# Scaling and sums of the down-projection weights: from one early block to short pieces placed along the feed-forward chunks

## The chip, the cores and the metric

The kernel runs on one core of a Trainium2 chip. The metric is the device time of one launch in microseconds (us). TensorE (PE) does the matmuls, VectorE (DVE), ScalarE (ACT) and GpSimd (POOL) do elementwise work, and SyncE (SP) issues nearly all the DMA transfers. The engines run side by side, each through its own list of instructions in a fixed order, and wait for each other through semaphores.

## The reference

One post-norm transformer layer on x of shape (2, 512, 512) in float32. The attention part is large; the change lies in the feed-forward part, whose weights come as int32 with a scale for each output:

```python
x = _layernorm(x + _L0_attn_ref(x, Wq, Wk, Wv, Wo, q_norm_w, k_norm_w))   # 32 heads, 8 kv heads, 128 wide
# feed-forward: D_MODEL = 512, D_FF = 1376
gate = silu(einsum('bsd,fd->bsf', x, gate_w.astype(f32)) * gate_s)
up   = einsum('bsd,fd->bsf', x, up_w.astype(f32)) * up_s
h    = gate * up
ffn  = einsum('bsf,df->bsd', h, down_w.astype(f32)) * down_s
x = _layernorm(x + ffn)
```

## The kernel before, in words

Both batches of 512 tokens stay in on-chip memory (SBUF) from start to end. Attention takes the first 80% of the time; from about 870 us on the feed-forward mixes in. Its gate and up projections are cut into 11 chunks of 128 features (the last has 96). Each chunk is computed for batch 0 and batch 1; "visit 9.1" below is chunk 9, batch 1. There are 22 visits: chunks 0 to 3 for batch 0, then chunks 4 to 10 for both batches, then chunks 0 to 3 for batch 1.

**Products.** A matrix product is done in a two-by-two block form with seven block products instead of eight (a Strassen-like scheme). Its operands are the blocks themselves and sums or differences of them. `PLAN` (line 546) lists the products in the order 1, 2, 6, 7, 4, 5, 3; they accumulate in three PSUM banks: 1, 6, 7 and 4 in bank a, 2 in bank c, 5 and 3 in bank b. After each product its bank is read out before the next product may write to it: `ffn_up` (line 1221) has ACT copy bank a into gu (line 640) and DVE add bank b or c to gu (`tensor`, line 513; line 518 in the profile). So product 6 waits for the copy after product 1, product 4 for the copy after product 7, and product 3 for the gu add after product 5, which itself needs the copy after product 7. When all seven are in, ACT computes the sigmoid (sg, line 1280) and DVE makes sg (line 1288) and hT (line 1297), the result of the visit. gu has two buffers: the first copy of a visit waits for hT of the visit before the last one.

**Operand sums.** For each chunk, the int32 weights wi come by DMA (line 1195), ACT or POOL cast them to wf, and four DVE or POOL operations make the weight sums sw (`sums_a`, line 523). wi, wf and sw have two buffers each. The sums over the tokens are tx. The down projection needs, for each pair of token tiles, sums sh over h, and once the differences td of its weights (`sums_b`, line 534): four operations on blocks of 5 chunks by 256 columns.

**Down weights.** They come as int32 in 11 pieces (wdi, line 1348, two buffers); DVE multiplies each by the output scale ds_sb into wd (128 x 512, in the loop of line 1342). Then `sums_b` makes td from wd in four operations of 1280 elements per partition. wd is first read by the down projection's products and by the 96-row rest (ps, line 1412), td by its later products.

**What sets the order.** The program doesn't write the order of the engines out by hand. Each operation is put on a list with an estimated cost for each engine that may do it, a priority, and the operations that it depends on. A planner (`Work.emit`, line 146) then plays the engines' clocks forward and emits at each step the operation that can start first, by estimated time and then by priority. The engine and the order are fixed by this at build time; the chip then only waits for data and for free buffers. An operation given in `after` counts as a dependence in the planner alone, and no semaphore comes of it. The estimates know nothing of engines slowing each other.

The priorities of the lines that change: the visits have `base + n` (n from 0 to 21), and

```python
base + 4.0 + fc      # load of wdi, piece fc
base + 4.5 + fc      # scaling of wd, piece fc
base + 16.0          # the four td differences
```

Of the kernel before, what the change touches and what calls it, by code (L numbers as in the profile page):

```python
# [26 lines left out]
NF = -(-DFF // P)  # L27
FL = DFF - (NF - 1) * P
KF = (NF - 1) // 2
# [3 lines left out]
WO = DM // 2  # L33
# [5 lines left out]
EARLY = 4  # L39
# [14 lines left out]
def act(n, scaled=False):  # L54
    return 0.15 + 0.00084 * n + (0.1 if scaled else 0.0)


def dve(n, sbuf=False):
    return 0.2 + 0.0014 * n if sbuf else 0.15 + 0.00106 * n


def pool_tt(n):
    return 0.28 + 0.0021 * n
# [168 lines left out]
def post_ln_block(  # L232
# [23 lines left out]
    W = Work()  # L256
# [18 lines left out]
    def fixed(ring_, name):  # L275
        return Buf(ring_, name)
# [51 lines left out]
    qw, kw = fixed(r_qw, "qw"), fixed(r_kw, "kw")  # L328
# [16 lines left out]

    def load(mb, prio, fn, writes, reads=(), queue="SP"):
        engine = {"SP": nc.sync, "ACTQ": nc.scalar}[queue]
        W.add({queue: mb / 0.3}, prio, lambda e: fn(engine), reads, writes)  # L350

    w_qkv, w_o = {}, {}

# [156 lines left out]

    def tensor(n, prio, dst, a, b, alu, reads, writes, who=("DVE", "POOL")):
        cost = {"DVE": dve(n, len(who) > 1), "POOL": pool_tt(n)}
        W.add(
            {e: cost[e] for e in who},
            prio,
            lambda e: vec[e].tensor_tensor(dst(), a(), b(), alu),  # L518
            reads,
            writes,  # L520
        )

    def sums_a(n, prio, s, a, s_key, a_keys):
# [7 lines left out]
        tensor(n, prio, g(1), g(0), f(0, 0), sub, [s_key(0)] + k(0, 0), [s_key(1)])  # L531
        tensor(n, prio, g(3), f(0, 1), g(1), sub, k(0, 1) + [s_key(1)], [s_key(3)])

    def sums_b(n, prio, t, b, t_key, b_keys):

        sub = ALU.subtract
        k = b_keys
        f = lambda r, c: (lambda: b(r, c))
        g = lambda j: (lambda: t(j))
        tensor(n, prio, g(0), f(0, 1), f(0, 0), sub, k(0, 1) + k(0, 0), [t_key(0)])  # L540
        tensor(n, prio, g(1), f(1, 1), g(0), sub, k(1, 1) + [t_key(0)], [t_key(1)])
        tensor(n, prio, g(2), f(1, 1), f(0, 1), sub, k(1, 1) + k(0, 1), [t_key(2)])
        tensor(n, prio, g(3), f(1, 0), g(1), sub, k(1, 0) + [t_key(1)], [t_key(3)])


    PLAN = [
# [90 lines left out]
    def copy_op(n, prio, dst, src, reads, writes, who=("ACT", "DVE")):  # L637
        def fn(e):
            if e == "ACT":
                nc.scalar.copy(dst(), src())  # L640
            else:
                vec[e].tensor_copy(dst(), src())  # L642

        cost = {"ACT": act(n), "DVE": dve(n), "POOL": 0.2 + 0.00095 * n}
        W.add({e: cost[e] for e in who}, prio, fn, reads, writes)
# [472 lines left out]
    for p in range(NP):  # L1118
        g, b, i = pairs[p]
# [96 lines left out]
        )  # L1216
        return wf, sw

    turn = [0]

    def ffn_up(fc, b, weights, prio):

        fw = min(P, DFF - fc * P)
        key = f"{fc}_{b}"
        wf, sw = weights
        gu, sg = Buf(r_gu, f"gu_{key}"), Buf(r_sg, f"sg_{key}")
        if b not in hT:
            hT[b] = Buf((r_h0, r_h1)[b], f"hT_{b}")
        h, xb, tb = hT[b], x1T[b], tx[b]
        homes = ((r_f, r_f, r_f), (r_sc, r_sc, r_po))[turn[0] % 2]  # L1230
        turn[0] += 1

        def copy(n, bank):
            copy_op(
                NTH,
                prio,
                lambda: gu[:fw, n, :],
                lambda: bank[:fw, :NTH],
                [A(bank)],
                [(gu, n)],  # L1240
                ("ACT",),
            )

        def add(n, bank):
            tensor(
                NTH,
                prio,
                lambda: gu[:fw, n, :],
                lambda: bank[:fw, :NTH],
                lambda: gu[:fw, n, :],  # L1250
                ALU.add,
                [A(bank), (gu, n)],
                [(gu, n)],
                ("DVE",),
            )

        def done(which, bank):
            if which == 1:
                copy(0, bank)
            elif which == 2:  # L1260
                add(0, bank)
            elif which == 6:
                copy(1, bank)
            elif which == 7:
                copy(3, bank)
            elif which == 5:
                add(3, bank)
            elif which == 4:
                copy(2, bank)
            else:  # L1270
                add(1, bank)
                finish()

        def finish():
            gcol, ucol = lambda: gs_sb[:fw, fc : fc + 1], lambda: us_sb[:fw, fc : fc + 1]
            gate = lambda: gu[:fw, 0:2, :].rearrange("p n c -> p (n c)")
            W.add(
                {"ACT": act(S, True)},
                prio,
                lambda e: nc.scalar.activation(sg[:fw, :], gate(), AF.Sigmoid, scale=gcol()),  # L1280
                [(gu, 0), (gu, 1), A(gs_sb)],
                [A(sg)],
                table="sigmoid",
            )
            W.add(
                {"DVE": 0.75},
                prio,
                lambda e: nc.vector.scalar_tensor_tensor(
                    sg[:fw, :], gate(), gcol(), sg[:fw, :], ALU.mult, ALU.mult
                ),  # L1290
                [(gu, 0), (gu, 1), A(gs_sb), A(sg)],
                [A(sg)],
            )
            W.add(
                {"DVE": 0.75},
                prio,
                lambda e: nc.vector.scalar_tensor_tensor(
                    h[:fw, fc, :],
                    gu[:fw, 2:4, :].rearrange("p n c -> p (n c)"),
                    ucol(),  # L1300
                    sg[:fw, :],
                    ALU.mult,
                    ALU.mult,
                ),
                [(gu, 2), (gu, 3), A(us_sb), A(sg)],
                [(h, (fc, 0)), (h, (fc, 1))],
            )

        def a_ap(f, ch):
            if isinstance(f, tuple):  # L1310
                return wf[:, f[0], 2 * f[1] + ch, :fw]
            return sw[:, f, ch, :fw]

        def a_keys(f):
            return [(wf, f[0])] if isinstance(f, tuple) else [(sw, f)]

        def b_ap(f, ch):
            if isinstance(f, tuple):
                return xb[:, 2 * f[0] + ch, f[1] * NTH : (f[1] + 1) * NTH]
            return tb[:, f, ch, :]  # L1320

        def b_keys(f):
            return [(xb, 2 * f[1]), (xb, 2 * f[1] + 1)] if isinstance(f, tuple) else [(tb, f)]

        seven(prio, Factor(a_ap, a_keys), Factor(b_ap, b_keys), fw, NTH, 2, f"h{key}", done, homes)


    base = NU + 3.0
# [3 lines left out]
    n = 0  # L1332
# [8 lines left out]
    wd, td = Buf(r_wd, "wd"), Buf(r_td, "td")  # L1341
    for fc in range(NF):
        fw = min(P, DFF - fc * P)
        wdi = Buf(r_wdi, f"wdi_{fc}")
        load(
            0.26,
            base + 4.0 + fc,
            lambda q, fc=fc, fw=fw, wdi=wdi: q.dma_start(
                wdi[:fw, :], dwt[fc * P : fc * P + fw, :]
            ),  # L1350
            [A(wdi)],
        )
        tensor(
            DM,
            base + 4.5 + fc,
            lambda fc=fc, fw=fw: wd[:fw, fc, :],
            lambda fw=fw, wdi=wdi: wdi[:fw, :],
            lambda fw=fw: ds_sb[:fw, :],
            ALU.mult,
            [A(wdi), A(ds_sb)],  # L1360
            [(wd, fc)],
            ("DVE",),
        )
    sums_b(
        KF * WO,
        base + 16.0,
        lambda j: td[:, j],
        lambda r, n: wd[:, KF * r : KF * r + KF, n * WO : (n + 1) * WO],
        lambda j: (td, j),
        lambda r, n: [(wd, KF * r + c) for c in range(KF)],  # L1370
    )

    def ffn_down(t, prio):
        b, i = divmod(t, NTB)
# [26 lines left out]
            return td[:, f, ch, :]  # L1401

        def b_keys(f):
            return [(wd, KF * f[0] + c) for c in range(KF)] if isinstance(f, tuple) else [(td, f)]


        for r in (0, 1):
# [4 lines left out]
                lambda e, r=r, bank=bank: nc.tensor.matmul(  # L1412
                    bank.tile,
                    lhsT=h[:FL, NF - 1, ts(i + r, P)],
                    rhs=wd[:FL, NF - 1, :],
                    start=True,
                    stop=True,
                ),
# [13 lines left out]
                ("DVE",),  # L1432
            )
        seven(prio, Factor(a_ap, a_keys), Factor(b_ap, b_keys), P, WO, KF, f"d{t}", done, homes)
        for r in (1, 0):
            o = Buf(r_o, f"o_{t + r}")
# [4 lines left out]
                lambda q, r=r, o=o: q.dma_start(out[ts(t + r, P), :], o.tile),  # L1441
# [54 lines left out]
```

## Time and profile before

| what | value |
|---|---|
| median of 3 runs | 1101.1 us (1099.43 to 1101.75) |
| the profiled execution's own time | 1100.44 us |
| its span, first to last instruction | 1098.5 us |
| mean granted PE clock | 0.995 |
| PE busy | 1073.0 us, 98% of the span |
| DVE, ACT, POOL busy | 676.1, 409.8, 485.2 us |
| scaling of wd on DVE | ten records of 128x512, 12.4 us in all, mean 1251 ns |
| td differences | three on POOL, mean about 3.1 us; one on DVE, 1.48 us |

The profile is of one execution. A line of the timeline gives start and length in us, the engine, the line of the source, the operation, the tile written and the tiles read, and in brackets the idle time before it with what ended it. "PEld" is PE's weight load. A matmul of one product of the feed-forward shows as four records in a row. A PE that is busy need not run at full speed: the granted clock is given beside it, with 1.00 as full.

### The profile page before, as it was taken

To read this page: it belongs to the slowest core of one execution; us is meant where nothing else is said; L and a number is where in the kernel's file an instruction comes from. 1 tells how busy PE (TensorE), PEld (TensorE's weight loads), DVE (VectorE), ACT (ScalarE), POOL (GpSimd) and SP (SyncE) were. 2 spreads that over 40 slices of the span, in tenths; PEclk is the share of its full clock that TensorE was granted. 3 is DMA by queue.
4 is the path that set the end of the run, shared out by engine and by line. 5 is a ranking of instruction groups with operands and counts; after the bars stand their busy time and mean duration, and the time that the engine had idled before them with its cause. 6 is when DMAs were issued, how large, how long until landed. Compare 5 with 4: busy or idle time off the path is not lost.

```text
span 1098.5 us, 13035 instructions
## 1 busy us (share of the span) xinstructions
PE 1073.0 (98%) x4548; PEld 764.7 (70%) x4548; DVE 676.1 (62%) x1553; ACT 409.8 (37%) x1015; POOL 485.2 (44%) x596
## 2 busy tenths in 40 slices
PE   8999999999999999999999999999999987999997
PEld 5667676767676666666676666666667775888886
DVE  8756565656564655465665656566666588557454
ACT  2543334344344434434333434344444332344100
POOL 9443444344543444335444445354656265224030
PEclk9999999999999999999999999999999998999999
DMA  9210011001100110011001100000101033111011
GB/s 281 74 58 1 1 39 58 1 1 39 58 1 1 38 58 1 1 39 58 1 1 39 58 1 16 23 1 1 39 1 39 20 88 92 33 40 38 1 39 39
DMA packets 44144, 38.92 MB, mean 35 GB/s; under 512 B 3664, under 2 KB 36432, under 8 KB 44080
## 3 DMA queue, kind: packets, MB, share of 16 engines
q1 hardware_dynamic: 42352, 37.05, 11.0%
q10 hardware_dynamic: 1728, 1.05, 0.4%
q8 instruction: 36, 0.59, 0.2%
q14 instruction: 28, 0.23, 0.1%
HBM read 35.99 MB, written 2.10 MB: 35 GB/s over the span
## 4 chain that ended last, share of the span: by engine, by line
PE 85%; DVE 7%; POOL 5%; DMA 1%; issue 1%; ACT 1%; SPq 0%; POOLq 0%; DVEq 0%
PE pa_q L565 13%; PE pa L965 10%; PE sc L874 10%; PE pa_o L565 9%; PE pt L942 6%; PE pb_q L565 6%; PE pa_h L565 6%; PE pb_o L565 5%; PE pc_q L565 4%; PE pb_h L565 3%; PE pa_d L565 3%; PE ptq L821 2%; DVE tq L518 2%; PE pc_o L565 2%; POOL inv L504 2%; POOL pr L923 2%
## 5 line engine op out<-in xcount | busy, mean ns | idle before, releaser
L923 POOL TENSOR_SCALAR pr<-pr,rden 128x32 f32<-128x32 f32 (+15 forms) x256 | 155.8, 627 | 148.6 <-DVE rden L914 148.0
L899 ACT ACTIVATE pr<-pr,nmax 128x32 f32<-128x32 f32 (+15 forms) x256 | 131.9, 516 | 95.4 <-DVE nmax L883 95.2
L965 PE MATMUL pa<-prT,v 128*128 128x512 f32 x320 | 164.2, 595 | 0.0
L874 PE MATMUL sc<-kT,qT 128*128 128x160 f32 (+15 forms) x512 | 149.0, 402 | 0.0
L883 DVE CUSTOM_DVE_ANT_0 pr<-sc,bias 128x32 f32<-128x32 f32 (+15 forms) x256 | 109.0, 436 | 28.0 <-PE sc L874 25.3
L874 PEld LDWEIGHTS sc<-kT,qT 128*128 128x128 f32 x512 | 90.4, 191 | 47.6 <-issue 29.6
L640 ACT COPY c<-pa_q 128x384 f32<-128x384 f32 x101 | 48.2, 477 | 135.4 <-PE pa_q L565 130.5
L942 PEld LDWEIGHTS pt<-ident,pr 128*128 128x128 f32 x640 | 76.4, 141 | 26.7 <-issue 9.7
L942 PE MATMUL pt<-ident,pr 128*128 128x128 f32 x640 | 91.5, 275 | 0.9 <-POOL pr L923 0.3
L565 PE MATMUL pa_q<-tq,sx 128*128 128x384 f32 x248 | 90.4, 487 | 1.4 <-POOL pr L923 1.4
L640 ACT COPY prT<-pt 128x512 f32<-128x512 f32 x107 | 60.4, 586 | 79.1 <-PE pt L942 79.0
L504 POOL TENSOR_TENSOR inv<-ms,nhalf 128x10 f32<-128x10 f32 x32 | 63.3, 1977 | 53.5 <-DVE ms L779 53.2
L518 DVE TENSOR_TENSOR y<-y,pa_o 128x256 f32<-128x256 f32 x128 | 53.6, 419 | 50.7 <-PE pa_o L565 49.9
L642 DVE COPY prT<-pt 128x512 f32<-128x512 f32 x53 | 36.2, 690 | 61.8 <-PE pt L942 61.7
L763 ACT ACTIVATE sq<-c 128x640 f32<-128x640 f32 x64 | 47.2, 737 | 69.6 <-DVE c L518 67.4
L518 DVE TENSOR_TENSOR c<-pb_q,c 128x384 f32<-128x384 f32 x62 | 34.3, 554 | 61.9 <-PE pb_q L565 58.1
L965 PEld LDWEIGHTS pa<-prT,v 128*128 128x128 f32 x320 | 56.7, 191 | 21.9 <-issue 4.9
L642 POOL COPY v<-c 128x128 f32<-128x128 f32 x50 | 16.1, 321 | 124.1 <-DVE c L518 124.1
L565 PE MATMUL pa_o<-to,so 128*128 128x256 f32 x256 | 65.9, 380 | 0.3 <-POOL pr L923 0.3
L565 PEld LDWEIGHTS pa_q<-tq,sx 128*128 128x128 f32 x248 | 46.0, 192 | 27.4 <-POOL pr L923 2.6
L565 PEld LDWEIGHTS pa_o<-to,so 128*128 128x128 f32 x256 | 47.1, 190 | 20.1 <-issue 9.9
L640 ACT COPY gu<-pa_h 128x256 f32<-128x256 f32 (+1 forms) x88 | 31.9, 370 | 78.1 <-PE pa_h L565 65.3
(152 smaller groups left out, 2060.3 us busy)
## 6 DMA issues: line engine op xcount, KB each, us to landing
w<-in_wqt_dram SPq DMA_DIRECT2D x32, 256.0 KB, 4.3
wo<-in_wot_dram SPq DMA_DIRECT2D x8, 1024.0 KB, 5.5
wi<-in_gwt_dram SPq DMA_DIRECT2D x14, 256.0 KB, 2.9
wi<-in_uwt_dram SPq DMA_DIRECT2D x14, 256.0 KB, 3.2
wdi<-in_dwt_dram SPq DMA_DIRECT2D x10, 256.0 KB, 2.7
y<-in_x_dram SPq DMA_DIRECT2D x1, 2048.0 KB, 13.1
out_dram<-o SPq DMA_DIRECT2D x8, 256.0 KB, 2.0
w<-in_wkt_dram SPq DMA_DIRECT2D x7, 256.0 KB, 4.9
```

Of the source, the lines that this page charges most:

```text
L504: lambda e: nc.gpsimd.tensor_tensor(dst(), src(), nhalf[:, :n], ALU.pow),
L518: lambda e: vec[e].tensor_tensor(dst(), a(), b(), alu),
L565: nc.tensor.matmul(bank[:rows, :width], lhsT=a(fa, c), rhs=b(fb, c), start=(fresh and c == 0), stop=(c == depth - 1), skip_group_check=True,)
L640: nc.scalar.copy(dst(), src())
L642: vec[e].tensor_copy(dst(), src())
L763: lambda e, r=r: nc.scalar.activation(sq[:, r].rearrange("p h d -> p (h d)"), c(r)[:, : 5 * HD], AF.Square),
L874: lambda e, a=a, w=w, sc=sc: nc.tensor.matmul(sc[:, :w], lhsT=qT[:, a, :, :], rhs=kT[:, :w], start=True, stop=True),
L883: lambda e, a=a, w=w, sc=sc: nc.vector.tensor_tensor_reduce(out=pr[:, a, :w], in0=sc[:, :w], in1=bg[:, S - w :], scale=-1.0, scalar=MAX_IN ...
L899: lambda e, a=a, w=w: nc.scalar.activation(pr[:, a, :w], pr[:, a, :w], AF.Exp, bias=nmax[:, a : a + 1], scale=-1.0, accum_out=den[:, a : a ...
L923: lambda e, a=a, w=w: nc.gpsimd.tensor_scalar(pr[:, a, :w], pr[:, a, :w], rden[:, a : a + 1], 1.0, ALU.mult, ALU.mult),
L942: nc.tensor.transpose(pt[:, ts(a, P)], pr[:, a, ts(j, P)], ident.tile)
L965: lambda e, j=j, prT=prT: nc.tensor.matmul(po.tile, lhsT=v[:, j, :], rhs=prT.tile, start=(j == 0), stop=(j == i)),
```

## The change

The planner is told more. Each wdi load and each wd scaling is held in the plan until a given visit is finished, and the td differences are cut from four operations of 5 x 256 into twenty of 256, four for each of five chunk pairs, each group held until a given visit is finished. `finished` collects, for each of the 22 visits, the operation that writes hT; `EARLY` is 4 and `NF` 11. So piece fc of wd may be planned once visit number 4 + fc (counted from 0) is done, its load one visit earlier, and group c of td once visit 15 + c is done. Besides, the cost that the planner assumes for a wd scaling is changed from that of a PSUM operation to that of an SBUF one (0.69 to 0.92 us by its formulas). The keys by which td's readers depend on it are made per group.

```diff
-    def load(mb, prio, fn, writes, reads=(), queue="SP"):
+    def load(mb, prio, fn, writes, reads=(), queue="SP", after=()):
         engine = {"SP": nc.sync, "ACTQ": nc.scalar}[queue]
-        W.add({queue: mb / 0.3}, prio, lambda e: fn(engine), reads, writes)
+        W.add({queue: mb / 0.3}, prio, lambda e: fn(engine), reads, writes, after)
...
-    def tensor(n, prio, dst, a, b, alu, reads, writes, who=("DVE", "POOL")):
-        cost = {"DVE": dve(n, len(who) > 1), "POOL": pool_tt(n)}
+    def tensor(n, prio, dst, a, b, alu, reads, writes, who=("DVE", "POOL"), sbuf=None, after=()):
+        cost = {"DVE": dve(n, len(who) > 1 if sbuf is None else sbuf), "POOL": pool_tt(n)}
...
-    turn = [0]
+    turn, finished = [0], []
...
                 [(gu, 2), (gu, 3), A(us_sb), A(sg)],
                 [(h, (fc, 0)), (h, (fc, 1))],
             )
+            finished.append(W.ops[-1])
...
     for fc in range(NF):
         fw = min(P, DFF - fc * P)
         wdi = Buf(r_wdi, f"wdi_{fc}")
+        pace = [finished[EARLY + fc]]
         load(
             0.26,
             base + 4.0 + fc,
...
             [A(wdi)],
+            after=[finished[EARLY + fc - 1]],
         )
         tensor(
             DM,
...
             ("DVE",),
-        )
-    sums_b(
-        KF * WO,
-        base + 16.0,
-        lambda j: td[:, j],
-        lambda r, n: wd[:, KF * r : KF * r + KF, n * WO : (n + 1) * WO],
-        lambda j: (td, j),
-        lambda r, n: [(wd, KF * r + c) for c in range(KF)],
-    )
+            sbuf=True,
+            after=pace,
+        )
+    for c in range(KF):
+        sums_b(
+            WO,
+            base + 16.0 + c,
+            lambda j, c=c: td[:, j, c],
+            lambda r, n, c=c: wd[:, KF * r + c, n * WO : (n + 1) * WO],
+            lambda j, c=c: (td, (j, c)),
+            lambda r, n, c=c: [(wd, KF * r + c)],
+            after=[finished[EARLY + NF + c]],
+        )
```

In the compiled program no engine's list differs before about 890 us of the profile. From there on the lists of DVE, POOL, ACT, SP and, by small swaps of neighbouring products, PE differ, since the planner decides anew with each change.

More of the change, by code (lines that the diff above doesn't have):

```diff
@@ L520, in tensor @@
             writes,
+            after,
         )
@@ L532, in sums_a, with sums_b @@
         tensor(n, prio, g(3), f(0, 1), g(1), sub, k(0, 1) + [s_key(1)], [s_key(3)])
-    def sums_b(n, prio, t, b, t_key, b_keys):
+    def sums_b(n, prio, t, b, t_key, b_keys, **kw):
         sub = ALU.subtract
@@ L539, in sums_b @@
         g = lambda j: (lambda: t(j))
[L540 to L543, printed above, removed]
+        tensor(n, prio, g(0), f(0, 1), f(0, 0), sub, k(0, 1) + k(0, 0), [t_key(0)], **kw)
+        tensor(n, prio, g(1), f(1, 1), g(0), sub, k(1, 1) + [t_key(0)], [t_key(1)], **kw)
+        tensor(n, prio, g(2), f(1, 1), f(0, 1), sub, k(1, 1) + k(0, 1), [t_key(2)], **kw)
+        tensor(n, prio, g(3), f(1, 0), g(1), sub, k(1, 0) + [t_key(1)], [t_key(3)], **kw)
     PLAN = [
@@ L1403, in b_keys @@
         def b_keys(f):
-            return [(wd, KF * f[0] + c) for c in range(KF)] if isinstance(f, tuple) else [(td, f)]
+            if isinstance(f, tuple):
+                return [(wd, KF * f[0] + c) for c in range(KF)]
+            return [(td, (f, c)) for c in range(KF)]
         for r in (0, 1):
```

## The prediction

> **What bounds the kernel now.** First the page: TensorE (PE) is the bound, and its few lost slices lie in the feed-forward, at 32 and 33 of 40 (879 to 934 us); section 2's two rows:
>
> ```profile
> PE   8999999999999999999999999999999987999997
> ...
> PEclk9999999999999999999999999999999998999999
> ```
>
> Next the busy time by stretch (length; busy us and records of PE, PEld, DVE, ACT, POOL; granted clock; DMA share; GB/s):
>
> ```profile
> 898.00:940.00 42.00, 33.65 (x132) 28.02 (x133) 33.23 (x41) 10.99 (x27) 21.00 (x16) 0.88 0.32 92
> 940.00:982.00 42.00, 42.00 (x196) 37.05 (x195) 22.17 (x41) 16.90 (x39) 10.87 (x15) 1.00 0.17 47
> 982.00:1003.00 21.00, 20.94 (x98) 16.58 (x97) 15.39 (x23) 8.69 (x20) 9.56 (x7) 1.00 0.09 26
> ...
> 912.00:917.00 5.00, 4.28 (x13) 3.56 (x14) 2.91 (x7) 1.09 (x2) 0.00 (x0) 0.66 0.24 57
> ...
> 930.00:937.00 7.00, 6.80 (x18) 5.50 (x19) 4.08 (x8) 1.36 (x3) 0.00 (x0) 0.55 0.01 2
> ```
>
> From 940 on PE runs full: 196 records in 42.00 us, 0.857 us for the four records of a product. At that rate the 132 records of 898 to 940 need 28.3 us, so this stretch loses 13.7 us: 8.35 us idle, and 5.4 us of matmuls at a lower clock (0.66, 0.55) just after. By the same count 890 to 898 (23 records, 8.00 us) loses 3.1 us. From 940 to the tail nothing is lost that could be won.
>
> What PE waits for between 900 and 940, from the view of waits (us, times, longest):
>
> ```profile
> PE pb_h L565 <- DVE gu L518: 8.1, 3, 4.5
> ```
>
> And the timeline at the two long ones (start, length, engine, what, idle before it):
>
> ```profile
> 908.37 3.32 POOL L518 TENSOR_TENSOR td<-wd 128x1280 f32<-128x1280 f32 x1 [0.63 <-DVE wd L518]
> ...
> 908.87 3.37 DVE L518 TENSOR_TENSOR wd<-wdi,ds_sb 128x512 f32<-128x512 int32 x1
> ...
> 912.16 0.41 DVE L518 TENSOR_TENSOR gu<-pb_h,gu 128x256 f32<-128x256 f32 x1
> ...
> 912.72 2.04 PE L565 MATMUL pb_h<-x1T,sw 128*128 128x256 f32 x4 [3.26 <-DVE gu L518]
> ...
> 915.14 0.68 DVE L518 TENSOR_TENSOR wd<-wdi,ds_sb 128x512 f32<-128x512 int32 x1
> ...
> 923.09 3.07 POOL L518 TENSOR_TENSOR td<-wd,td 128x1280 f32<-128x1280 f32 x1
> ...
> 926.11 3.06 POOL L518 TENSOR_TENSOR td<-wd 128x1280 f32<-128x1280 f32 x1
> ...
> 926.36 3.36 DVE L1288 SCALAR_TENSOR_TENSOR sg<-gu,gs_sb,sg 128x512 f32<-128x512 f32 x1
> ...
> 930.20 2.04 PE L565 MATMUL pb_h<-x1T,sw 128*128 128x256 f32 x4 [4.50 <-DVE gu L518]
> ```
>
> A wd scaling takes 0.68 us alone (915.14) but 3.37 us beside a 1280-wide td difference on POOL: it ends 0.55 us after POOL's. Behind it in DVE's order stands gu<-pb_h, which frees the bank that product 3 writes. So wd on DVE and td on POOL, together, stop PE twice.
>
> **The skill.** The Trainium skill, SBUF — State Buffer, Who interferes with whom: a DVE instruction with two SBUF inputs and a GpSimd instruction that reads SBUF exclude each other, and the later one waits out the earlier. The trace agrees; adds that read PSUM keep their 0.41 to 0.43 us. TensorE: Matmul & The Clock Gate, What's actually happening: after an idle window of about 3.4 us the array runs at half clock. Here 3.26 and 4.50 us idle were followed by it, 1.15 us (before 895.65) was not.
>
> **Part 1, the burst goes.** The eleven wd scalings keep size and engine; in the compiled order they stand one per visit from chunk 4, batch 0 (written 4.0) to 9.0, each after that visit's hT. The four td differences of 1280 (three on POOL, 9.45 us; one on DVE, 1.48) become twenty of 256: nine on POOL, eleven on DVE, from 9.1 to 2.1. Like ones, sw, take 0.41 us on DVE and 0.73 on POOL alone: 4.5 and 6.6 us. Both parts leave 895 to 936. Walked with the trace's durations, the new order gives at 4.0: product 7 ends 906.7, ACT's copy (0.37) 907.1, the gu add 907.6; product 3 is due at 908.2. Nothing there holds PE, so all of the 13.7 us goes. Of the 3.1 us before it, the wait on hT (1.15) stays; without wd at 895.06 and 897.07, product 3 of 2.0 waits about 0.4 us less, and that of 3.0 (0.37 now, plus its restart) not at all: 0.9. Sum: 14.6 us gained.
>
> **Part 2, wd inside the visits.** In steady state DVE idles 0.6 to 1.05 us between hT and the gu add of product 5 (0.71 at 944.25, 1.05 at 950.29), and product 3 starts 0.70 us after that add. A wd of 0.68 fits, or delays the add by about 0.15: nothing. Without that cover each wd would cost 0.68. At 5.0 the planner put product 6 of 5.1 ahead of product 3 of 5.0; ACT's copy behind hT of 4.1 is then about 0.45 us late for product 4; 8.0 has the same by 0.1. Cost 0.5 us.
>
> **Part 3, a new collision at chunk 10.** sh, the sums over h for the down projection, is dealt out anew: POOL had four sh_2 and DVE four sh_0; now POOL takes two early ones, then three sh_0, one sw, one sh_2 and td pieces in a row while DVE takes two sh_2. The trace today:
>
> ```profile
> 989.93 2.00 POOL L518 TENSOR_TENSOR sh<-hT,sh 128x640 f32<-128x640 f32 x1
> ...
> 992.14 1.21 DVE L1288 SCALAR_TENSOR_TENSOR sg<-gu,gs_sb,sg 128x512 f32<-128x512 f32 x1
> ...
> 993.27 0.41 DVE L518 TENSOR_TENSOR sw<-sw,wf 128x256 f32<-128x256 f32 x1
> ...
> 993.60 0.74 DVE L1297 SCALAR_TENSOR_TENSOR hT<-gu,us_sb,sg 128x512 f32<-128x512 f32 x1
> ...
> 994.43 0.73 ACT L640 COPY gu<-pa_h 96x256 f32<-96x256 f32 x2 [0.99 <-DVE hT L1297]
> ```
>
> On this clock the two orders run level until sg of 9.1 ends at about 993.3. Then POOL's sh_2 holds the port 1.4 us (an sh of 2.18 us at 985.58, less its wait for DVE until 986.35) to 994.7; sw, +0.35, 995.05; td on POOL, 0.55, 995.6; hT of 9.1 ends 0.56 after, 996.2, not 994.34. Behind hT waits ACT's first gu copy of 10.1 (0.37, to 996.6), and product 6 of 10.1 waits for that copy. In PE's new order product 6 stands two places earlier, at 993.73 instead of 995.73. It starts at 996.7: PE stands 2.96 us. Four products on, the same set of work is 2.7 us later than today. Idle before it is about 2.8 us, between the 1.15 that left the clock alone and the 3.26 that halved it; the two half-clock stretches cost 1.6 and 3.1 us (2 and 4 products at 0.864 took 3.32 and 6.53). Bounds 0 to 3.1; I take 1.0. Sum 3.7 us.
>
> **Part 4, the later td visits.** Each of 10.0 to 2.1 gets about four pieces. Walking 0.1 and 1.1 so, the gu add lands 8.5 against 8.65 needed and 14.5 against 14.65 (us after 1000): about 0.15 us spare. I take nothing; if POOL is slower, up to 0.5 each over four visits: 2. td is complete by about 1021 on today's clock, and first read at 1030.26: 9 us spare; the shift takes both along.
>
> **SP and DMA.** The eleven wdi loads (2.7 us to land) move behind later wi loads and wait for DVE to free one of two buffers. wi for chunk 9 stands behind wdi_3, which is free by 5.0; wi's own wait, the casts of chunk 7, ends later. Each wdi is issued about 6 us before its wd. Nothing. `after` only delays the planner's choice; the compiled td pieces wait for data alone, so no engine waits on it.
>
> **Sum.** 14.6 - 0.5 - 3.7 = 10.4 us. All of it is on PE's chain inside the span (1098.5 us); the 1.9 us around the span stay. From the profiled execution's own 1100.4 us: 1090.0. The median of the three runs is 0.7 us above that execution: 1090.7.
>
> **Rivals.** (a) The port is not passed on so strictly at chunk 10: DVE keeps it for sw and hT, hT of 9.1 ends at 994.34 as now, the copy at about 994.8, and only product 6's earlier place is left: 994.9 for 993.73, 1.1 us, no clock lost: 14.6 - 0.5 - 1.1 = 13.0 off, 1088.1. For: the page itself calls spans on POOL rough. Against: at 892.88 to 896.81 (tx on POOL; sg, hT and wd on DVE) the port went over at each end. (b) td visits and wd visits all leak: fifteen visits at 0.2 to 0.45 us, 3 to 7 us more: 1094 to 1098. For: 0.15 us of spare. Against: PE lost nothing in 940 to 1003 with POOL beside it. (c) The pieces run together all the same, since `after` makes no semaphore: 1101. Against: gu adds and hT stand between them in each engine's order. (d) Slower: in the td visits hT is late as at chunk 10, with the clock halved: 2.96 + 1.6 = 4.6 us each. 14.1 us of gain is eaten by three, so it decides from the fourth of five: five give 1110. For: the same POOL-DVE alternation. Against: POOL's long sh ends with 9.1; a 256 piece holds DVE 0.55 us.
>
> **Chances.** Forecast 0.45 (own range 1089 to 1093: half-clock cost 0 to 3.1 about the 1.0), (a) 0.24, (b) 0.21, (c) 0.04, (d) 0.06. The range 1086.3 to 1096 covers the forecast, (a) with 1.8 us to spare below it for a larger gain, and half of (b). Less than 0.2% (2.2 us) can't be told from no change. Faster 0.90 is the forecast, (a) and (b); same 0.04 is (c); slower 0.06 is (d).
>
> **What would show it.** Right: no 3 us wd or sg; the 3.26 and 4.50 us waits on gu gone, clock 1.00 in what is now 898 to 940; td as twenty of about 0.4 to 0.9 us; a PE wait of about 3 us on ACT's gu copy at chunk 10, some 14 us earlier than today's 993.7. Wrong: PE waits at each visit's product 3, SP waits of wi behind wdi, or PE waiting for td or sh in the down projection.

## The result, and the profile after

The changed kernel takes 1091.17 us (median of four runs, 1089.43 to 1093.10), the kernel before beside it on the same chip 1100.26 us (1099.26 to 1101.75): ratio 0.9917, 95% interval 0.9895 to 0.9938. Measured again later, beside two other kernels, it took 1091.14 us, ratio 0.9915 (0.9901 to 0.9928).

| | before | after |
|---|---|---|
| the profiled execution's own time, us | 1100.44 | 1091.2 |
| span, us | 1098.5 | 1089.1 |
| first matmul of the feed-forward, us | 845.76 | 846.42 |
| first matmul of a down-projection bank pa_d, us | 1025.95 | 1016.54 |
| end of the last matmul, us | 1092.50 | 1083.09 |
| DVE, POOL busy, us | 676.1, 485.2 | 670.2, 481.3 |

From the first feed-forward matmul to the first pa_d the stretch went from 180.19 to 170.12 us, 10.07 us less; from there to the last matmul it is 66.55 us in both. The start of the feed-forward came 0.66 us later, in a part of the program that the change does not touch (its first product stands near 846, earlier than the 870 given above, where the bulk of it begins). So the whole difference lies in the 22 visits.

The page's two rows for PE, now without the weak slices 32 and 33:

```profile
PE   8999999999999999999999999999999999999997
...
PEclk9999999999999999999999999999999999999999
```

Busy time by stretch (length; busy us and records of PE, PEld, DVE, ACT, POOL; granted clock; DMA share; GB/s):

```profile
898.00:930.00 32.00, 32.00 (x150) 28.17 (x149) 21.35 (x38) 13.94 (x32) 13.30 (x14) 1.00 0.35 100
930.00:970.00 40.00, 40.00 (x187) 35.21 (x186) 24.88 (x45) 15.49 (x36) 7.68 (x11) 1.00 0.27 81
...
976.00:984.00 8.00, 5.46 (x24) 3.79 (x23) 7.89 (x12) 1.62 (x4) 6.62 (x7) 0.93 0.25 66
984.00:992.00 8.00, 8.00 (x34) 6.03 (x33) 3.99 (x8) 2.97 (x7) 1.62 (x3) 0.86 0.00 0
```

PE is full from 898 to 970 at clock 1.00; in the part of it from 898 to 940 the kernel before lost 13.7 us. The loss that is left lies at 976 to 992, chunk 10. All waits of PE from 890 to 1012, from the view of waits (us in all, times, longest), and the timeline around the long one (start, length, engine, what, idle before it):

```profile
PE pa_h L566 <- ACT gu L641: 4.6, 4, 2.5
```

```profile
896.31 1.13 PE L566 MATMUL pa_h<-tx,sw 128*128 128x256 f32 x4 [1.14 <-ACT gu L641]
...
912.24 0.69 DVE L518 TENSOR_TENSOR wd<-wdi,ds_sb 128x512 f32<-128x512 int32 x1
...
978.95 1.98 POOL L518 TENSOR_TENSOR sh<-hT,sh 128x640 f32<-128x640 f32 x1
...
979.45 1.75 DVE L518 TENSOR_TENSOR sw<-sw,wf 128x256 f32<-128x256 f32 x1
980.89 0.90 POOL L518 TENSOR_TENSOR td<-wd 128x256 f32<-128x256 f32 x1
981.13 1.21 DVE L1298 SCALAR_TENSOR_TENSOR hT<-gu,us_sb,sg 128x512 f32<-128x512 f32 x1
...
982.45 0.64 ACT L641 COPY gu<-pa_h 96x256 f32<-96x256 f32 x2 [4.39 <-DVE hT L1298]
...
982.87 2.02 PE L566 MATMUL pa_h<-tx,sw 128*96 128x256 f32 x4 [2.54 <-ACT gu L641]
...
984.68 1.80 PE L566 MATMUL pa_h<-tx,wf 128*96 128x256 f32 x4
```

The chain is the one that the prediction walked: POOL's sh ends at 980.93, DVE's sw 0.27 us later, POOL's td at 981.79, and DVE's hT of 9.1 0.55 us after that; behind hT comes ACT's first copy of 10.1, and product 6 of 10.1 has waited 2.54 us. This product and the next take 1.81 and 1.64 us from start to start instead of 0.86: half clock. The three short waits at 892 to 896 (0.49, 0.46, 1.14 us) are in both kernels. A wd scaling has one length now, 0.68 us (11 records, 677 to 686 ns).

### The profile page after: what moved, and what is told of

Its sections match the earlier page's. It is cut to its first block, busy times and chain, and to the rows that moved or that the text cites. A ratio compares the mean times of both kernels' runs of the same rounds, so it can differ in the third digit from the quotient of the medians.

```text
span 1089.1 us, 13052 instructions
## 1 busy us (share of the span) xinstructions
PE 1070.1 (98%) x4548; PEld 762.2 (70%) x4548; DVE 670.2 (62%) x1563; ACT 411.4 (38%) x1017; POOL 481.3 (44%) x600
## 4 chain that ended last, share of the span: by engine, by line
PE 86%; DVE 5%; POOL 5%; DMA 2%; ACT 1%; issue 1%; SPq 0%; POOLq 0%; DVEq 0%; ACTq 0%
PE pa_q L566 13%; PE pa L966 10%; PE sc L875 10%; PE pa_o L566 9%; PE pa_h L566 6%; PE pt L943 6%; PE pb_q L566 6%; PE pb_o L566 5%; PE pc_q L566 4%; PE pa_d L566 3%; PE pb_h L566 3%; PE ptq L822 2%; DVE tq L518 2%; PE pc_o L566 2%; POOL inv L504 2%; POOL pr L924 2%
```

## The experiments

Each run is compared with the kernel before on its own chip. Since executions of one kernel differ by up to 5.3 us (1097.25 to 1102.55 for the kernel before in one set) and the question is about 1 to 4 us, the profiles are compared too, in one measure that doesn't see the start of the program: the time from the first feed-forward matmul to the end of the last matmul ("stretch"; in e8 and e12 the first pa_d stands 1.7 us earlier in PE's order, so that the expectations' measure, the time to that matmul, is not the same there). It is one profile for each run. The waits are those of PE on the feed-forward banks after 897 us, without the three short ones that all kernels have. A half-clock spell is a time within the stretch in which the granted clock was 0.50. In the column td stand the number of operations and whether they are held until late visits, not tied to a visit, or early as before; wd is either paced, one scaling for each visit, or in its early burst.

| run | td | wd | median us | ratio, 95% interval | stretch us | PE waits us | half-clock spells |
|---|---|---|---|---|---|---|---|
| before | 4 whole, early | early | 1100.26 | | 246.74 | 0.58, 0.37, 3.26, 4.50 | after 3.26 and 4.50 |
| after | 20, late | paced | 1091.17 | 0.9917 (0.9895 to 0.9938) | 236.67 | 2.54 | 1 |
| e1 | 4 whole, not tied | paced | 1089.40 | 0.9908 (0.9888 to 0.9928) | 235.42 | 0.96, 0.48, 1.02 | 0 |
| e2 | 20, not tied | early | 1095.54 | 0.9961 (0.9950 to 0.9973) | 240.08 | 1.00, 2.03, 1.96 | 1 |
| e3 | 20, late | early | 1094.37 | 0.9948 (0.9931 to 0.9964) | 236.99 | 0.58, 0.37, 0.57, 2.01 | 0 |
| e4 | as after, sh split | paced | 1090.04 | 0.9913 (0.9894 to 0.9933) | 235.05 | 0.38, 1.47 | 0 |
| e5 | 20, two visits later | paced | 1090.43 | 0.9919 (0.9896 to 0.9941) | 236.64 | 2.08 | 1 |
| e6 | e4 and e5 together | paced | 1089.61 | 0.9913 (0.9891 to 0.9935) | 234.57 | 0.37, 1.00 | 0 |
| e7 | 4 whole, early, DVE alone | early | 1088.82 | 0.9910 (0.9884 to 0.9937) | 235.06 | 0.58, 0.37, 0.57 | 0 |
| e8 | as before | early, estimate changed | 1099.26 | 0.9996 (0.9985 to 1.0007) | 244.47 | 0.27, 0.61, 1.59, 1.32, 3.33, 1.68 | 1 |
| e9 | the changed kernel again | paced | 1091.14 | 0.9915 (0.9901 to 0.9928) | 238.41 | 2.56 | 2 |
| e10 | e7 again | early | 1088.92 | 0.9902 (0.9886 to 0.9917) | 235.06 | 0.58, 0.37, 0.57 | 0 |
| e11 | 20, earlier, DVE alone | paced | 1092.11 | 0.9924 (0.9911 to 0.9938) | 236.02 | 3.25 | 0 |
| e12 | 4 whole, not tied, DVE alone | paced | 1087.97 | 0.9891 (0.9874 to 0.9907) | 234.23 | 1.78 | 0 |

Two theories were tried first. The port theory, that of the prediction: DVE's scalings and POOL's td hold each other up at the shared port. Its rival: eleven scalings within 40 us are simply too much for DVE (backlog).

### Which half of the change carries the gain: e1, e2, e3

e1 puts the four td differences of 1280 back, untied:

```diff
-    for c in range(KF):
-        sums_b(
-            WO,
-            base + 16.0 + c,
...
-            after=[finished[EARLY + NF + c]],
-        )
+    sums_b(
+        KF * WO,
+        base + 16.0,
...
+    )
```

> The changed kernel with its td put back to four differences of 1280 without pacing; the wd scalings stay one per visit. Port theory (a long td on POOL holds the SBUF port, and DVE's instruction beside it stretches to 3.3 us): the compiled order still has two td of 1280 on POOL, one behind the sums of chunk 7 and one behind those of chunk 10. Each should show a DVE instruction of about 3 us beside it and stop PE by 1 to 4.5 us, restart included; 1092 to 1098 us. Backlog theory (eleven wd scalings of 0.68 us in 40 us are too much for DVE, whatever POOL does): with wd spread out nothing is left to stop PE, and the collision of sh and td at chunk 10 is gone as well; 1086 to 1088 us.

Measured: 1089.40 us, between the two numbers; neither theory's was right. A td of 1280 on POOL did stretch DVE's instruction beside it, as the timeline shows:

```profile
966.38 2.89 POOL L518 TENSOR_TENSOR td<-wd,td 128x1280 f32<-128x1280 f32 x1 [1.23 <-DVE wd L518]
...
966.67 3.95 DVE L518 TENSOR_TENSOR td<-wd 128x1280 f32<-128x1280 f32 x1
...
970.54 0.41 DVE L518 TENSOR_TENSOR gu<-pb_h,gu 128x256 f32<-128x256 f32 x1
...
972.02 1.13 PE L566 MATMUL pa_h<-tx,sw 128*128 128x256 f32 x4 [0.96 <-ACT gu L641]
```

A td of 1.48 us alone takes 3.95 here. But only gu adds and a last td were queued behind it, no wd, sw or sg, and PE lost 0.96 us, not 3. The other whole td on POOL (2.91 us, at 935.7) cost PE nothing. How much a long hold costs depends on what else DVE has to do in that visit. And cutting td into twenty is not what the gain needs: with td whole the stretch is 1.2 us shorter than after, whose profile has one half-clock spell, worth 1.7 us, where that of e1 has none.

e2 keeps td cut but ties nothing, and the planner's estimate for wd is again that of before (the lines of the wdi load, of wd and of td go):

```diff
-            after=[finished[EARLY + fc - 1]],
...
-            sbuf=True,
-            after=pace,
...
-            after=[finished[EARLY + NF + c]],
```

> The changed kernel with the wd scalings and the td pieces tied to nothing: td stays cut into twenty of 256, and everything runs early in one burst as before, POOL and DVE sharing the pieces. Port theory (length of the POOL instruction decides): no DVE instruction beside a piece can be held much over 1.2 us; the two long PE waits on gu (3.26 and 4.50 us) shrink to below 1.5 us each and the clock stays at 1.00, so at least 10 of the 13.7 us of 898 to 940 come back; and product 6 of 10.1 stands where it did before, so chunk 10 costs nothing: 1087 to 1091 us. Backlog theory: DVE has the same wd burst and six pieces of td more; the waits stay at 3 us or over: 1098 to 1102 us.

Measured: 1095.54 us, between the theories again. The two long waits shrank from 3.26 and 4.50 to 2.03 and 1.96 us, not below 1.5:

```profile
907.52 1.21 DVE L518 TENSOR_TENSOR wd<-wdi,ds_sb 128x512 f32<-128x512 int32 x1
...
908.65 1.21 DVE L1298 SCALAR_TENSOR_TENSOR hT<-gu,us_sb,sg 128x512 f32<-128x512 f32 x1
...
909.28 1.17 POOL L518 TENSOR_TENSOR td<-wd 128x256 f32<-128x256 f32 x1
909.79 1.21 DVE L518 TENSOR_TENSOR wd<-wdi,ds_sb 128x512 f32<-128x512 int32 x1
...
911.48 1.41 PE L566 MATMUL pb_h<-x1T,sw 128*128 128x256 f32 x4 [2.03 <-DVE gu L518]
```

Short pieces bound one hold to 0.5 us (1.21 instead of 0.68 to 0.74), but now three DVE operations in a row are held, by td and sw on POOL, ahead of one gu add. It is the sum of the holds ahead of the gu add in its visit that PE sees, not the longest one.

e3 leaves the wd burst and its estimate as they were before and only cuts and ties td:

```diff
-            after=[finished[EARLY + fc - 1]],
...
-            sbuf=True,
-            after=pace,
```

> The changed kernel with the wd scalings tied to nothing (one burst at chunks 1 to 4, as before), the td pieces cut and tied. Port theory: with no td on POOL between 895 and 936 each wd takes about 0.7 us, up to 1.3 beside a weight sum of POOL; PE waits at most 1 us at a time there, 12 to 13.7 us come back; product 6 of 10.1 stands where it did before: 1087 to 1090 us. Backlog theory: the burst of wd alone keeps most of the waits: 1097 to 1102 us.

Measured: 1094.37 us median, 1091.42 in the profiled execution. In the burst the port theory holds: eleven scalings within 895 to 922, and PE's waits are 0.58, 0.37 and 0.57 us. Backlog is out. But its total was missed: a wait of 2.01 us stands at chunk 10, on DVE's gu add for product 3 of 10.0, behind hT of 9.1, which was late as in the changed kernel. The expectation had looked only at where product 6 stands. The profiled execution is the fastest of the six, with a mean granted clock of 0.999. The other five have 0.995 to 0.997. One spell of 3.4 us at half clock lowers the mean over the span by about 0.0016 and costs about 1.7 us, so by this estimate they fit one to three spells more than the profiled one; where these stood was not traced.

So in the profiled executions either half carries nearly all of the gain (stretch 11.3 us shorter with wd paced alone, 9.7 with td cut and tied alone, 10.1 with both). In the medians this holds for pacing wd (10.3 us below the kernel before), while cutting and tying td has 5.3 us. The two are substitutes, since each takes wd and td apart, but with the second the waits of the burst stay (0.58, 0.37 and 0.57 us).

### The port by itself: e7, e10, and the estimate alone: e8

e7 is the kernel before with one argument more; no operation is paced or cut. With one engine to choose from, the planner also takes 1.5 us for such a td on DVE where it took 2.0.

```diff
     sums_b(
         KF * WO,
         base + 16.0,
...
         lambda r, n: [(wd, KF * r + c) for c in range(KF)],
+        who=("DVE",),
     )
```

> The kernel before, with its four td differences of 1280 on DVE alone, so that the burst and all its work stay, DVE gets 4.5 us more of it and POOL loses 9.5 us. Port theory: no wd or sg of 3 us is left; a td of 1.5 us on DVE delays a gu add by 0.8 us at most; PE's waits between 895 and 940 are below 1 us each, and the feed-forward stretch takes 168 to 173 us instead of 180.2: 1089 to 1094 us. Backlog theory: DVE has more to do in the same 40 us, PE's waits on gu stay at 3 us or grow: 1100 us or more.

Measured: 1088.82 us, and 168.51 us to the first pa_d, as the port theory expected; the time is just below its 1089 to 1094 us. From the windows and the timeline of e7, in the stretch where the kernel before lost 13.7 us:

```profile
898.00:940.00 42.00, 40.80 (x186) 35.05 (x187) 34.84 (x53) 15.14 (x37) 19.03 (x20) 1.00 0.36 105
```

```profile
908.87 0.68 DVE L518 TENSOR_TENSOR wd<-wdi,ds_sb 128x512 f32<-128x512 int32 x1
...
910.14 1.48 DVE L518 TENSOR_TENSOR td<-wd 128x1280 f32<-128x1280 f32 x1
```

The wd at 908.87 took 3.37 us in the kernel before, at the very same time. DVE is busier than there (34.84 us against 33.23 of 42) and does 53 records instead of 41, yet PE has 186 records instead of 132 at clock 1.00. The cause of the stall is shown: it is POOL's td beside DVE, and DVE has room for the wd burst and td together.

e8 has one other edit alone, the planner's estimate for a wd scaling:

```diff
             ("DVE",),
+            sbuf=True,
         )
```

> The kernel before with one edit of the change alone: the planner's estimate of a wd scaling is that of an operation that shares the port; nothing is tied or cut. All theories: the burst stays, with wd and td of full length beside each other; PE's waits on gu stay in sum within 3 us of today's 8.1, and the feed-forward stretch takes 177 to 182 us. If it is 172 us or less, the planner's estimate and not the ties carries the gain.

Measured: 1099.26 us, ratio 0.9996; its PE waits on the bank that DVE reads sum to 7.9 us:

```profile
PE pb_h L566 <- DVE gu L518: 7.9, 4, 3.3
```

The time to the first pa_d was 176.19 us, a little under the 177 to 182 expected. The stretch in its one profile is 2.3 us shorter (the waits fall elsewhere and only one is followed by a spell of half clock); the medians show no gain. The estimate does not carry it.

e10 measures e7 again, next to e9.

> The kernel before with td on DVE alone, measured again. If that one edit is worth as much as the whole change or more (168.5 us of feed-forward in its first profile against 170.1): ratio 0.988 to 0.991, and a time 1 to 2.5 us below the changed kernel's. If its first times were luck of the first 40 us of the program, where runs differ by 2 us: no difference.

Measured: 1088.92 us, the stretch 235.06 us as in e7. Against the changed kernel beside it, 2.2 us less in the median; the intervals of the two ratios (0.9886 to 0.9917 and 0.9901 to 0.9928) overlap.

### The collision at chunk 10: e4, e5, e6

e4 deals sh out as the kernel before had it, the early sh_0 to DVE and sh_2 to POOL (`who` is handed through `sums_a`):

```diff
         sums_a(
             KF * P,
             prio - 0.5,
...
             lambda r, k: for_half(k),
+            ("DVE",) if t == 0 else ("POOL",) if t == 2 else ("DVE", "POOL"),
         )
```

> The changed kernel with the four early sh_0 given to DVE alone and the four sh_2 to POOL alone. In the compiled order sh and td no longer stand in a row on POOL at chunk 10, and product 6 of 10.1 stands behind products 4 and 3 of 10.0. Theory of the chunk 10 collision: PE's wait of 2.5 us on ACT's gu copy there is gone, and the 1.7 us of half clock behind it: 4.2 us off the changed kernel's 1091.2, less up to 0.5 where an sh of 1.3 us on DVE delays a gu add: 1087.0 to 1087.8 us. Rival (POOL has the port as long as before, the stall only moves): 1090 to 1092 us.

Measured: 1090.04 us; the stretch is 1.6 us shorter, where 4.2 was expected. The wait on ACT's copy fell to 0.38 us and the half clock is gone, but another took its place:

```profile
984.21 1.07 PE L566 MATMUL pb_h<-x1T,sw 128*96 128x256 f32 x4 [1.47 <-DVE gu L518]
```

That is product 3 of 10.0, whose gu add stands behind hT of 9.1 on DVE. hT is still late (POOL: three sh, two sw, td), and the product that meets it is a different one, since the planner orders the products anew. Half of the rival, "the stall only moves", is right.

e5 moves td two visits on and leaves sh:

```diff
-            after=[finished[EARLY + NF + c]],
+            after=[finished[EARLY + NF + c + 2]],
```

> The changed kernel with each group of td pieces tied two visits later (after 10.1 to 3.1 instead of after 9.1 to 2.1); the order of sh and the place of product 6 of 10.1 stay. In the changed kernel's trace POOL's td piece of 0.90 us at 980.89 lies between the sh of 1.98 us and hT of 9.1. If td is the smaller part of the stall at chunk 10: hT of 9.1 ends about 0.45 us earlier, PE still waits about 2.1 us on ACT's gu copy, and the half clock behind it stays or goes (a wait of 2.03 us was followed by it in one trace, waits of 1.96 and 2.01 us were not): from the first matmul of the feed-forward to the first of the down projection 169.7 or 168.0 us instead of 170.1. If td is the larger part: a wait below 1 us and 166.9 us or less. Either way td must be there in time for the down projection's first read, 4 us after its first matmul; a PE wait there would say it is not.

Measured: 1090.43 us. From the timeline of e5:

```profile
980.48 0.74 DVE L1298 SCALAR_TENSOR_TENSOR hT<-gu,us_sb,sg 128x512 f32<-128x512 f32 x1
...
981.75 1.93 PE L566 MATMUL pa_h<-tx,sw 128*96 128x256 f32 x4 [2.08 <-ACT gu L641]
```

(In the changed kernel the last group is tied to visit 1.1, here to 3.1.) td was the smaller part, 0.46 of the 2.54 us; hT is back to 0.74 us and only the sh and sw ahead of it are left. The half clock stayed. The stretch to the first pa_d is 169.70 us, as expected in that branch. PE did not wait for td in the down projection, though its last group now stands after visit 3.1.

e6 is both edits.

> Both edits at once: sh_0 on DVE and sh_2 on POOL alone, and each td group two visits later. If the collision at chunk 10 is made of sh and td together, and each edit alone leaves one of them: PE waits at most 0.5 us there, no half clock, the feed-forward stretch takes 166.2 us (the changed kernel's 170.1 less its 2.5 us wait and 1.7 us of half clock, and what is left of 0.4), and the kernel about 1086.5 to 1087.5 us. If POOL's weight sums are enough by themselves to hold hT of 9.1: a wait of 1 us or more stays, and 1088 to 1090 us.

Measured: 1089.61 us, stretch 234.57, waits 0.37 and 1.00 us. The collision is made of sh, sw and td, and taking td out and splitting sh brings it from 2.54 us with half clock to 1.37 without; the expected 0.5 was not reached, and the other branch, a wait of 1 us that stays and 1088 to 1090 us, came. In this profiled execution the clock was 0.84 from 30 to 40 us, far from any edit, and the feed-forward began at 848.53 us, 2.7 us later than in e1; that is why its own time (1091.03 us) is above the median.

### What a version without td on POOL can reach: e11, e12

e11 is the changed kernel with the pieces on DVE alone and tied four visits earlier:

```diff
-            after=[finished[EARLY + NF + c]],
+            who=("DVE",),
+            after=[finished[EARLY + 7 + c]],
```

> The changed kernel with the td pieces on DVE alone and each group tied four visits earlier (after 7.1 to 9.1), so that no td is on POOL and most of td is done before chunk 10. Theory (td on POOL beside DVE's hT is what costs at chunk 10, and a piece of 0.41 us on DVE fits beside a wd): the 2.5 us wait becomes 1 us or less, no half clock, the feed-forward stretch takes 165.5 to 167.5 us: 1086.5 to 1088.5 us. Rival (twenty pieces of 0.41 us on DVE, three or more behind each other, make gu adds late): waits of 0.5 to 1 us at product 3 of 8.1 to 10.0, 168 to 170 us: 1089 to 1091 us.

(Group 0 moves from visit 15 to visit 11 counted from 0, so "four earlier".) Measured: 1092.11 us. Both expectations fell; the rival's 168 to 170 us to the first pa_d did come (169.47), but by a wait that it did not name. No gu add was late at 8.1 or 9.0, but at chunk 10 a wait of 3.25 us came:

```profile
979.67 1.98 POOL L518 TENSOR_TENSOR sh<-hT,sh 128x640 f32<-128x640 f32 x1
...
980.18 1.75 DVE L518 TENSOR_TENSOR td<-wd,td 128x256 f32<-128x256 f32 x1
981.61 1.71 POOL L518 TENSOR_TENSOR sh<-sh,hT 128x640 f32<-128x640 f32 x1
981.85 2.02 DVE L1298 SCALAR_TENSOR_TENSOR hT<-gu,us_sb,sg 128x512 f32<-128x512 f32 x1
...
984.35 1.07 PE L566 MATMUL pb_h<-x1T,sw 128*96 128x256 f32 x4 [3.25 <-DVE gu L518]
```

Here the planner gave POOL six sh at chunk 10, with one weight sum among them, presumably since td filled DVE's estimated time. A td piece of 0.41 us on DVE takes 1.75 beside one of them, and hT 2.02. So it isn't td on POOL alone that costs at chunk 10; a row of sh on POOL does the same.

e12 is e1 with td on DVE alone.

> The wd scalings one per visit as in the changed kernel, and the four td differences whole, tied to nothing, on DVE alone. It asks what pacing wd adds once no td is on POOL. With td on DVE and wd early PE still waited 0.58, 0.37 and 0.57 us on gu (168.5 us of feed-forward). If pacing adds: those three waits go, and 166.5 to 167.5 us. Against it: in the compiled order two td of 1.48 us stand in a row ahead of a gu add of product 5 in chunk 9, so that product 3 there waits about 1.4 us, and POOL has four sh in a row against two on DVE at chunk 10, worth 0.5 to 3 us of waiting: then 168.5 to 171 us and no gain over 1088.9 us.

Measured: 1087.97 us, ratio 0.9891 (0.9874 to 0.9907), the lowest median of all. The three waits of e7 are gone:

```profile
898.00:940.00 42.00, 42.00 (x196) 36.95 (x196) 29.27 (x51) 18.20 (x42) 15.45 (x17) 1.00 0.31 90
```

The wait of 1.4 us feared in chunk 9 did not come (two td of 1.48 us at 966.55 and 967.95, the gu add at 969.35, PE without a wait); at chunk 10 there is one of 1.78 us, again product 3 of 10.0 behind hT (2.02 us beside sh). The stretch is 2.4 us shorter than after. Three of its four runs (1087.83 to 1088.07) lie below all eight runs of the changed kernel in the two sets (1089.28 to 1093.10), the fourth, at 1090.04, does not; the intervals of the ratios overlap. From e7 (1088.82 us, 0.9884 to 0.9937) the medians do not tell it apart; its stretch is 0.8 us shorter in one profile of each.

### The changed kernel again: e9

> The changed kernel as it is, measured again beside the two below on one chip. Ratio to the kernel before 0.989 to 0.994. In its profile the 2.5 us wait and the half clock at chunk 10 should be there again at the same product, and the feed-forward stretch should take 170.1 us within 0.2: both are set by the order of the instructions, not by chance.

Measured: 1091.14 us. The wait at chunk 10 is there at the same product, 2.56 us. But the part to the first pa_d took 171.86 us, 1.74 more than in the first profile, though every wait is equal. The difference is here. In the first profile the products after the wait of 1.14 us start 0.97 and 0.86 us apart; here 1.33 us, and the next at 898.89, 1.71 us on:

```profile
895.85 1.54 PE L566 MATMUL pa_h<-tx,sw 128*128 128x256 f32 x4 [1.15 <-ACT gu L641]
...
897.18 1.91 PE L566 MATMUL pa_h<-tx,wf 128*128 128x256 f32 x4
```

The same three short waits were followed by half clock in this execution and in no other that was profiled. "Set by the order of the instructions, not by chance" was right for the wait and wrong for the clock.

## Why the prediction was right, and where its terms were off

The mechanism and the direction were right, and the forecast of 1090.7 us is 0.5 from the median. That it is so near is in part luck: it started from 1101.1 us, the median of three runs, while the four beside the changed kernel have 1100.26, so that the medians gained 9.1 us (6.8 to 11.6 by the interval) where 10.4 was forecast. Against the profiled execution: 1090.0 forecast, 1091.2 measured, of which 0.66 us lies before the feed-forward. In the stretch to the first pa_d 10.4 us were forecast and 10.07 came.

- **Part 1, the burst goes: 14.6 forecast, 14.5 measured**, as a remainder (the 10.07 and what chunk 10 now costs, 4.44, below). PE is full from 898 to 970. The term was put together with a flaw: the wait of 0.37 us at 903.15 was counted within the 13.7 us of 898 to 940 and again in the 0.9 us ahead of it. The walk of 4.0 held: nothing holds product 3 there. Ahead of 898, the way from the wait on hT to product 3 of 2.0 shrank from 2.58 us (895.65 to 898.23) to 1.83 (896.31 to 898.14), 0.75 us of the 0.9, where 0.4 was forecast for it; this and the double count nearly cancel, which is luck too.
- **The cause.** "wd on DVE and td on POOL, together, stop PE twice" is shown by e7 (td off POOL, the rest left) and by e3 (td away in time). What the Trainium skill says in SBUF — State Buffer, Who interferes with whom, that a DVE operation with two inputs in SBUF contends with a GpSimd operation that reads SBUF, agrees with this: with POOL's td gone, 3.37 us at 908.87 became 0.68. The prediction did not ask whether cutting was needed; e1 and e2 say that it is neither needed nor enough.
- **Part 2, wd inside the visits: 0.5 forecast, nothing measured.** PE has no wait between 898 and 980. What this term had wrong is the two visits where the planner had swapped neighbouring products: the copies were not late enough to be seen.
- **Part 3, the new collision: 3.7 forecast, 4.44 measured.** The chain was right link by link: td 0.59 us and hT 0.55 us after it (0.55 and 0.56 forecast). PE's wait was 2.54 us, not 2.96; the distance from product 2 of 10.1 to product 6 (979.30 to 982.87) is 2.71 us more than the 0.86 of full rate, so the wait with its restart cost the 2.7 us of the forecast. Half clock took 1.73 us more (982.87 to 987.19 for three products, 4.32 us for 2.59), where 1.0 was chosen out of bounds of 0 to 3.1. That term is the largest miss, 0.7 us; its bounds came from the lengths of two waits, and the last section shows that the length of one wait does not decide. e5 sizes td's part, 0.46 us.
- **Part 4, later td visits: nothing forecast, nothing measured.** The twenty pieces take 0.41 to 1.17 us; td is complete at 1009.2 and first read at 1020.6, 11 us spare.
- **SP and DMA: nothing, and nothing is seen.** wdi lands in 3.3 us instead of 2.7.
- **Rivals.** (a) fell: the port went over at each end, hT was late. (b) and (d) fell: the td visits cost nothing. (c) fell: the pieces do not run together.
- **What would show it** was seen as written: no wd or sg of 3 us, no wait of 3.26 or 4.50 us, clock 1.00, and the wait on ACT's copy at chunk 10, which begins at 980.3 us, 13.4 us ahead of 993.7 where 14 was written.

## What to carry to other kernels

When two engines share a port, look for what is queued behind the held instruction, and first try to give the whole operation to one of them: here one argument, td on DVE alone, was worth as much as cutting and pacing, and with wd paced as well it has the lowest median seen (1087.97 us, not told apart from 1088.82). Cutting an operation short bounds each hold, but the holds ahead of one wait add up; and whatever a planner is told about one operation, it deals out the others anew, so look next at the place where the row of work on the slower engine now ends (sh at chunk 10 in most versions here).

## What the runs showed of the hardware that was not expected

- **Half clock is not decided by the length of one wait, but by idle time within a window of fixed place.** In these traces it followed waits of 2.03, 2.08, 2.54, 2.56, 3.26, 3.33 and 4.50 us, and once a row of 0.50, 0.46 and 1.15 us within 4.4 us; it did not follow 1.96, 2.01 or 3.25 us, nor the same row in the other profiles. The prediction had set a limit between 1.15 and 3.26 us; there is none that fits. The traces keep the moments at which the granted clock changed. In each of the fourteen profiles they lie whole multiples of 3.413 us apart, from the first to the last (in e9, 896.43, 899.84, 985.17 and 988.59: 1, 26 and 27 of them after the first). A spell lasted one such window, two after the wait of 4.50 us; one window costs about 1.7 us. Read by these windows, first e9, then e11, whose places follow from its changes at the two ends of the trace:

```profile
893.01:896.43 3.42, 1.81 (x8) 1.21 (x8) 3.42 (x6) 1.02 (x3) 1.78 (x2) 1.00 0.02 5
896.43:899.84 3.41, 3.41 (x10) 2.70 (x9) 0.17 (x1) 1.08 (x3) 0.61 (x1) 0.50 0.00 0
...
979.17:982.58 3.41, 1.93 (x9) 1.14 (x7) 3.41 (x3) 0.37 (x1) 3.41 (x3) 1.00 0.25 72
982.58:986.00 3.42, 1.66 (x8) 1.32 (x9) 3.42 (x5) 0.64 (x2) 2.60 (x2) 1.00 0.00 0
986.00:989.41 3.41, 3.41 (x17) 2.55 (x16) 3.13 (x7) 1.08 (x3) 0.00 (x0) 1.00 0.00 0
```

The 3.25 us of e11 are cut in two by the end of a window, 1.48 and 1.76 us idle, and no half clock follows. In e9 1.61 us of the row fall into one window; in the first profile of the same kernel they fall into two, 0.96 and 1.14 us. Over all windows between the first feed-forward matmul and the last matmul, in all fourteen profiles, each with 2.03 us or more of idle PE was followed by half clock, and none with up to 1.78 us was, that one of 1.61 us apart. So about half a window idle decides, and for a wait of around 2 to 3 us the place of the window; what exactly is counted stays open. The Trainium skill, TensorE: Matmul & The Clock Gate, What's actually happening, gives a window of 3413 ns that does not begin anew with the kernel, and half clock after an idle window. Length and free place of the window agree with the traces; but a window need not be idle throughout, since 2.03 us of it were enough.
- **This explains part of the spread.** Executions of one kernel with equal waits differ by 1.7 us for each such spell (e9 against after; the profiles of e4 and e6 have a low clock between 20 and 40 us). The fastest execution of the changed kernel in e9, 1089.28 us, and that of e10, 1088.43 us, both at a mean clock of 0.999, are 0.9 us apart, where the medians of the two are 2.2 apart. Differences of 1 to 2 us between kernels are read better from a stretch of the traces, with the spells counted apart, than from the medians of a few runs.
- **A held DVE operation ends a time after POOL's that depends on its own size alone:** sg, hT and wd of 512 elements 0.54 to 0.55 us after the end of the POOL operation that held them, sw and td of 256 elements 0.27 to 0.29 us, sh of 640 elements 0.68 us and the td of 1280 in e1 1.35 us, whether POOL's operation was one of 256, 640 or 1280 elements.
